# Splitting the accumulating expert scatters of the last 22 tiles into two column halves

## The chip, the cores and the metric

The kernel runs on one core of one Trainium2 chip. The metric is the device time of one launch in microseconds (us). The engines of the core are named as in the profile: PE (TensorE) multiplies matrices, PEld is its weight load, DVE (VectorE) and ACT (ScalarE) work elementwise, POOL (GpSimd) here issues the indirect DMAs, and SP (SyncE) issues the plain ones. An indirect DMA takes an index for each of the 128 partitions and writes that partition's row to the row of a DRAM tensor that the index names; with an add as its compute operation it adds the row to what stands there.

## What is computed

A tokenizer turns the input into 4 x 64 x 64 = 16384 tokens of 256 columns. One attention layer with decay and one MLP follow, and then a mixture of 8 experts, of which every token uses its best two:

```python
logits = tokens @ router_w.T
probs = softmax(logits)
rw, re = top_k(probs, 2);  rw = rw / rw.sum(-1)
combine = zeros(N, E); combine[arange(N), re] = rw
out = tokens
for e in range(8):
    h = gelu(tokens @ w1[e] + b1[e])
    y = h @ w2[e] + b2[e]
    out = out + combine[:, e:e+1] * y
```

The reference evaluates all experts for all tokens; the kernel gathers, for each expert, only the tokens that chose it. Each token's row of the output so receives two additions from expert work, from two different experts, and with that from two different tiles.

## The kernel before

**Blocks.** The tokens are worked on in 32 blocks of 512 (`BLK`), numbered by `Block.i`; `NS` is 31, so the last block is number 31. In one turn of the main loop three blocks are in flight: one is embedded, the middle one goes through attention and MLP, the oldest is routed. When a block is routed, its MLP output is stored to `out` (`Block.store`, the store is kept as `self.stored`), and each token's row of 260 four-byte words (the 256 columns and four words with weights and the token's number) is scattered to `xbuf`, a DRAM buffer with a region for each expert (`Block.scatter`, L814 to L829, a plain indirect DMA at L819).

**Tiles.** After a block is placed, `take` (L858) turns the rows that have piled up into `Tile` objects: 256 rows of one expert. There are 131 of them. The last but one take makes 4 tiles (from block 29), the last take 18 (from block 30). The last block's tokens are not scattered: all 8 experts run on all of them (`Expert`, L1058), and the results are combined in the buffer `h` and stored at the end (L1115).

**A tile's stages.** `load` fetches the expert's weights and the rows, `turn` rearranges them, `enter` (L997) does the first product and the gelu, `leave` (L1014) the second product into a PSUM buffer of the pool `p_tm` (three buffers), and `sums` (L1027) finishes: DVE adds the bias (L1036, out of PSUM into `y`, of which pool `four` has four buffers), multiplies by the token's share (L1038, twice), for the last take's tiles also computes `known` (L1043, the row numbers with the rows that another tile already handled turned away), and then POOL issues two indirect DMAs with an add, one for each 128 of the 256 rows (L1048). `Expert` does the same for the last block with `enter` (L1076, product at L1081) and `leave` (L1092, product at L1098, DVE at L1106 and L1112).

**What sets the order.** SP, PE, DVE and ACT run in the order in which the kernel's source issues the work (`MANUAL`); POOL is not in that list, the compiler's planner places its instructions. Toward the end the loop alternates: an `expert_step` of a tile, a piece of the last block's MLP, another tile; and after the MLP, tiles and the eight `Expert` objects in turn.

**The order of the additions.** An accumulating DMA reads the destination and writes it back. Two tiles of different experts may hold the same token. So the kernel declares the tensor `out` free of automatic dependencies (`unordered`) and states the needed ones itself: both scatters of a tile wait until both scatters of the tile before (`added[-2:]`) and the store of the block (`self.block.stored`) have landed. The scatters of all tiles so form one chain.

Of the kernel before, what the change touches and what calls it, by code (L numbers as in the profile page):

```python
# [13 lines left out]
I32 = mybir.dt.int32  # L14
# [3 lines left out]
ALU = mybir.AluOpType  # L18
AX = mybir.AxisListType

P = 128
# [15 lines left out]
def vit_tower_kernel(  # L37
# [15 lines left out]
    nc = tc.nc  # L53
    B, NBLK, _, XW = x.shape
    D = wtok.shape[2]
# [22 lines left out]
    NS = NB - 1  # L78
# [17 lines left out]
    sums = [p_g.tile([P, BLK], F32, name=f"sums{i}") for i in range(3)]  # L96
# [17 lines left out]
    with tc.tile_pool(name="prep", bufs=1) as prep:  # L114
# [19 lines left out]
        for j in range(J):  # L134
            ps = p_mm.tile([P, 2, D], F32, name="mm")
            for odd in range(2):
                for k in range(CH):
                    n = (odd * CH + k) * 2
# [74 lines left out]
    twelve = ctx.enter_context(tc.tile_pool(name="twelve", bufs=12))  # L213
# [627 lines left out]
    def after(what, others):  # L841
        for other in others:
            tc.add_manual_dep(
                what.ins,
                other.ins.name,
                mybir.DependencyInfo(mybir.DependencyClass.Sync, mybir.DependencyReason.DATA),
                reason="rows",
            )

    def unordered(name, what, others):  # L850

        tc.declare_no_dep(what.ins, group=name, keep=[o.ins for o in others], reason="rows of their own")
        after(what, others)
        tc.add_to_no_dep_group(name, what.ins)
# [93 lines left out]
    AHEAD = 4  # L948
    last_product = [None]
    tiles = []  # L950
    added = []

    class Tile:

# [72 lines left out]
        def sums(self):  # L1027
            w, ps = self.w, self.ps
            share = small.tile([P, 2], F32, name="tile_share")
            tag = w[:, 5 * D + KD : 5 * D + KD + 1]  # L1030
            nc.vector.scalar_tensor_tensor(
                share, self.xg.bitcast(F32)[:, :, FIRST - D], tag, self.xg.bitcast(F32)[:, :, DIFF - D], ALU.is_equal, ALU.mult
            )
            nc.vector.tensor_tensor(share, share, self.xg.bitcast(F32)[:, :, SECOND - D], ALU.add)
            y = four.tile([P, 2, D], F32, name="y")
            nc.vector.tensor_tensor(y, ps, w[:, 4 * D : 5 * D].unsqueeze(1).to_broadcast([P, 2, D]), ALU.add)  # L1036
            for c in range(2):
                nc.vector.tensor_scalar(y[:, c, :], y[:, c, :], share[:, c : c + 1], None, ALU.mult)  # L1038

            number = self.xg[:, :, NUMBER - D : NUMBER - D + 1]  # L1040
            if self.done is not None:
                known = twelve.tile([P, 2, 1], I32, name="known")
                nc.vector.tensor_tensor(known[:, :, 0], number[:, :, 0], self.done[:, self.t, :], ALU.max)  # L1043
                number = known

            before = added[-2:] + [self.block.stored]
            for c in range(2):
                add = nc.gpsimd.indirect_dma_start(  # L1048
                    out=out,
                    out_offset=bass.IndirectOffsetOnAxis(ap=number[:, c, :], axis=0),  # L1050
                    in_=y[:, c, :],
                    in_offset=None,
                    compute_op=ALU.add,
                )
                unordered("sums", add, before)
                added.append(add)

    class Expert:  # L1058

# [63 lines left out]
    at = dict(load=0, fetch=0, turn=0, enter=0, leave=0, sums=0)  # L1123
# [34 lines left out]
    def slot_halves(known, load=True, sums=True):  # L1158

        if len(tiles) - at["enter"] > LEFT and at["enter"] + 2 <= known:  # L1160
            yield from expert_halves(load=load, sums=sums)
# [299 lines left out]
```

## Time and profile before

| | |
|---|---|
| median of three runs | 2114.51 us |
| lowest and highest run | 2113.27 and 2120.39 us |
| the profiled execution's own time | 2116.49 us |
| its span in the profile | 2114.7 us |
| granted TensorE clock | 0.994 |
| busy: PE / PEld / DVE / ACT / POOL | 98% / 75% / 79% / 52% / 42% |
| accumulating scatters (L1048) | 226 + 36 |

The profile is one execution. The span runs from the first to the last instruction; the execution's time has 1.8 us more. Times inside the profile are given from the start of the span. The busy times of the page are over the whole span; since stages differ, what counts here is the last 150 us, for which the trace was asked separately. The profiled duration of an indirect DMA on POOL is the engine's own work on it, not the movement of the data. The name that stands after "<-" for the releaser of a wait is inferred, and where it names an instruction that plainly ended by chance at that moment, the real one is another.

### The profile page before, as it was taken

To read this page: it belongs to the slowest core of one execution; us is meant where nothing else is said; L and a number is where in the kernel's file an instruction comes from. 1 tells how busy PE (TensorE), PEld (TensorE's weight loads), DVE (VectorE), ACT (ScalarE), POOL (GpSimd) and SP (SyncE) were. 2 spreads that over 40 slices of the span, in tenths; PEclk is the share of its full clock that TensorE was granted. 3 is DMA by queue.
4 is the path that set the end of the run, shared out by engine and by line. 5 is a ranking of instruction groups with operands and counts; after the bars stand their busy time and mean duration, and the time that the engine had idled before them with its cause. 6 is when DMAs were issued, how large, how long until landed. Compare 5 with 4: busy or idle time off the path is not lost.

```text
span 2114.7 us, 30454 instructions
## 1 busy us (share of the span) xinstructions
PE 2077.4 (98%) x9042; PEld 1576.0 (75%) x9042; DVE 1674.8 (79%) x5179; ACT 1100.8 (52%) x1966; POOL 886.9 (42%) x768
## 2 busy tenths in 40 slices
PE   8999999999999999999999999999999999998999
PEld 5777677777777777777777777787777787676776
DVE  6778888888888888888888888888888888767445
ACT  2344455655545565554556555455665545543453
POOL 1032234444444444544444444444444444535444
PEclk9999999999999999999999999999999999999999
DMA  4031256766676676567667766766776567688653
GB/s 142 4 123 64 80 131 138 160 143 129 134 157 146 155 160 139 125 143 159 156 143 160 150 122 136 157 156 143 163 157 118 138 149 161 138 197 168 91 69 50
DMA packets 424519, 283.21 MB, mean 134 GB/s; under 512 B 355104, under 2 KB 391072, under 8 KB 420256
## 3 DMA queue, kind: packets, MB, share of 16 engines
q1 hardware_dynamic: 373424, 208.35, 42.5%
q0 software_dynamic: 49632, 67.39, 17.8%
q10 hardware_dynamic: 1296, 5.52, 0.8%
q8 instruction: 71, 1.16, 0.2%
q14 instruction: 96, 0.79, 0.1%
HBM read 118.36 MB, written 86.52 MB: 97 GB/s over the span
## 4 chain that ended last, share of the span: by engine, by line
PE 74%; DVE 11%; ACT 5%; DMA 5%; issue 2%; POOL 2%; SPq 1%; another core or an unknown queue 0%; ACTq 0%; DVEq 0%; POOLq 0%
PE tm L650 17%; PE sums L339 13%; PE tm L396 9%; PE sums L524 9%; PE mm L1002 8%; PE tm L1019 8%; DMA turned<-planes 3%; DVE st L263 2%; PE mm L540 1%; ACT planes L318 1%; ACT tokT L332 1%; PE tm L1098 1%; PE mm L1081 1%; PE mm L539 1%; SPq L326 1%
## 5 line engine op out<-in xcount | busy, mean ns | idle before, releaser
L1048 POOL DMA_INDIRECT out<-y,xg x226 | 369.2, 1634 | 432.7 <-DVE y L1038 220.2
L650 PE MATMUL tm<-w_sb,aT 128*128 128x256 f32 x2048 | 454.7, 380 | 0.0
L339 PE MATMUL sums<-hT,w_sb 128*128 128x512 f32 x1024 | 451.7, 593 | 1.3 <-ACT aT L640 1.3
L650 PEld LDWEIGHTS tm<-w_sb,aT 128*128 128x128 f32 x2048 | 386.7, 190 | 57.2 <-DVE z L611 4.8
L819 POOL DMA_INDIRECT xbuf<-row,to x248 | 257.1, 1037 | 294.3 <-DVE ks L560 170.5
L339 PEld LDWEIGHTS sums<-hT,w_sb 128*128 128x128 f32 x1024 | 193.4, 190 | 219.9 <-issue 201.0
L396 PE MATMUL tm<-wu,xv 128*128 128x256 f32 x1280 | 282.5, 379 | 0.0
L318 ACT COPY planes<-zz 128x1024 uint16<-128x1024 uint16 x100 | 99.3, 1041 | 342.0 <-DVE zz L292 342.0
L396 PEld LDWEIGHTS tm<-wu,xv 128*128 128x128 f32 x1280 | 242.7, 190 | 32.7
L1002 PE MATMUL mm<-xT,w 128*128 128x256 f32 x1048 | 252.5, 384 | 6.9 <-ACT xT L995 3.8
L1019 PE MATMUL tm<-w,ge 128*128 128x256 f32 x1048 | 253.4, 385 | 0.0
L1002 PEld LDWEIGHTS mm<-xT,w 128*128 128x128 f32 x1048 | 201.3, 193 | 49.9 <-issue 16.0
L1019 PEld LDWEIGHTS tm<-w,ge 128*128 128x128 f32 x1048 | 195.9, 191 | 31.4 <-issue 2.9
L640 ACT ACTIVATE aT<-sums,vec 128x512 f32<-128x512 f32 x256 | 167.0, 690 | 60.6 <-PE sums L339 59.3
L995 ACT COPY xT<-xh 128x512 uint16<-128x512 uint16 x262 | 182.1, 767 | 24.4 <-DMA xh<-xbuf 15.4
L283 POOL TENSOR_SCALAR rstd<-mv 128x4 f32<-128x4 f32 x62 | 42.0, 678 | 333.2 <-DVE mv L264 296.7
L1010 ACT ACTIVATE ge<-mm,w 128x256 f32<-128x256 f32 x262 | 109.9, 474 | 137.5 <-PE mm L1002 76.3
L1036 DVE TENSOR_TENSOR y<-tm,w 128x512 f32<-128x512 f32 x131 | 90.6, 691 | 97.9 <-PE tm L1019 86.6
L332 ACT COPY hT<-turned 128x512 uint16<-128x512 uint16 x100 | 66.2, 762 | 80.5 <-DMA turned<-planes 80.5
L263 DVE BATCH_NORM_STATS2 st<-h 128x6 f32<-128x256 f32 x256 | 104.8, 409 | 3.3
L332 ACT COPY tokT<-turned 128x512 uint16<-128x512 uint16 x116 | 76.5, 760 | 58.7 <-DMA turned<-row 58.7
L524 PE MATMUL sums<-hT,wqkv_sb 128*128 128x256 f32 x360 | 107.1, 379 | 0.0
(224 smaller groups left out, 3105.4 us busy)
## 6 DMA issues: line engine op xcount, KB each, us to landing
w<-in_wex SPq DMA_DIRECT2D x113, 641.5 KB
xb<-in_x SPq DMA_DIRECT2D x32, 1040.0 KB
out<-h SPq DMA_DIRECT2D x31, 512.0 KB
bank<-in_wex ACTq DMA_DIRECT2D x8, 641.5 KB
xbuf<-row,to POOLq DMA_INDIRECT x248
out<-y,xg POOLq DMA_INDIRECT x226
xh<-xbuf SPq DMA_TRANSPOSE x131
xg<-xbuf SPq DMA_DIRECT2D x131, 4.0 KB
```

The costliest lines, as they stand in the source:

```text
L263: nc.vector.bn_stats(self.st[:, t, :], src[:, t, :])
L332: copy(to[:, 1 - i], self.turned[:, :, i, k, :])
L339: nc.tensor.matmul(ps, lhsT=w[:, k, ts(m, P)], rhs=rhs[:, k, :], start=k == 0, stop=k == KD - 1)
L396: nc.tensor.matmul(ps[:, n, :], lhsT=xv[:, i, j, :], rhs=wu[:, i, j, :], start=j == 0, stop=j == J - 1)
L524: nc.tensor.matmul(g[:, n, :], lhsT=lhsT, rhs=rhs, start=False, stop=True, skip_group_check=True)
L640: nc.scalar.activation(self.aT[:, m, :], ps, AF.Relu, bias=vec[:, MB1 + m : MB1 + m + 1])
L650: last_product[0] = nc.tensor.matmul(ps[:, i, :], lhsT=self.aT[:, k, ts(u * 2 + i, P)], rhs=w2_sb[:, k, :], start=k == 0, stop=k == KH - 1,)
L819: write = nc.gpsimd.indirect_dma_start(out=xbuf, out_offset=bass.IndirectOffsetOnAxis(ap=self.to[:, c, t : t + 1], axis=0), in_=self.row[: ...
L995: nc.scalar.copy(halves[:, :, :, 1 - i], self.xh[:, i * KD : (i + 1) * KD, :])
L1002: nc.tensor.matmul(ps[:, m, :], lhsT=self.w[:, k * D + m * P : k * D + (m + 1) * P], rhs=self.xT[:, k, :], start=k == 0, stop=k == KD - 1,)
L1019: last_product[0] = nc.tensor.matmul(ps[:, c, :], lhsT=self.ge[:, k, ts(c, P)], rhs=w[:, (2 + k) * D : (3 + k) * D], start=k == 0, stop=k ...
L1048: add = nc.gpsimd.indirect_dma_start(out=out, out_offset=bass.IndirectOffsetOnAxis(ap=number[:, c, :], axis=0), in_=y[:, c, :], in_offset= ...
```

## The change

The tiles of the last two takes (blocks 29 and 30, so 22 of the 131) no longer issue two scatters of 128 rows x 256 columns, but four of 128 rows x 128 columns. For them `out` is viewed as twice as many rows of 128 columns, and two small DVE instructions compute the row numbers of the two halves (2n and 2n + 1). The two scatters of one half wait for the two scatters of the same half of the tile before, no longer for the other half. All other tiles do what they did.

```diff
-    added = []
+    added = [[], []]
...
-            before = added[-2:] + [self.block.stored]
-            for c in range(2):
-                add = nc.gpsimd.indirect_dma_start(
-                    out=out,
-                    out_offset=bass.IndirectOffsetOnAxis(ap=number[:, c, :], axis=0),
-                    in_=y[:, c, :],
-                    in_offset=None,
-                    compute_op=ALU.add,
-                )
-                unordered("sums", add, before)
-                added.append(add)
+            parts = 2 if self.block.i >= NS - 2 else 1
+            if parts == 2:
+                at = twelve.tile([P, 2, 2], I32, name="at")
+                for j in range(parts):
+                    nc.vector.tensor_scalar(at[:, j, :], number[:, :, 0], 2.0, float(j), ALU.mult, ALU.add)
+            befores = [added[j] + [self.block.stored] for j in range(2)]
+            for j in range(parts):
+                adds = []
+                for c in range(2):
+                    index = number[:, c, :] if parts == 1 else at[:, j, c : c + 1]
+                    add = nc.gpsimd.indirect_dma_start(
+                        out=out.rearrange("n (j d) -> (n j) d", j=parts),
+                        out_offset=bass.IndirectOffsetOnAxis(ap=index, axis=0),
+                        in_=y[:, c, ts(j, D // parts)],
+                        in_offset=None,
+                        compute_op=ALU.add,
+                    )
+                    unordered("sums", add, befores[j])
+                    adds.append(add)
+                added[j] = adds
+            if parts == 1:
+                added[1] = added[0]
```

## The prediction

> **What bounds the kernel now.** I read first the busy shares and the end of the chain of waits, then POOL's instructions in order of time, because the change touches only what POOL issues and what waits for it.
>
> ```profile
> PE 2077.4 (98%) x9042; PEld 1576.0 (75%) x9042; DVE 1674.8 (79%) x5179; ACT 1100.8 (52%) x1966; POOL 886.9 (42%) x768
> ```
>
> ```profile
> 2103.07 6.93 PE tm L1098 x32
> ...
> 2110.03 0.70 DVE zz L1106
> ```
>
> The first fence is the page's busy share, the second two steps of the chain that ended last (start, duration, what). PE is busy nearly everywhere, and from 2009.97 to 2110.0 the chain is PE without a gap. Then come the last block's DVE additions, its store, and the span's end at 2114.7. POOL isn't on this chain. So a scatter that lands earlier cannot, by itself, end the kernel earlier.
>
> Next, POOL at the end of the kernel (start, duration, operation, idle before).
>
> ```profile
> 1966.44 1.54 POOL L1048 DMA_INDIRECT out<-y,xg  x1 [3.28 <-DMA out<-y,xg]
> 1968.29 1.54 POOL L1048 DMA_INDIRECT out<-y,xg  x1 [0.30 <-issue]
> ...
> 2060.08 1.54 POOL L1048 DMA_INDIRECT out<-y,known  x1 [3.04 <-DVE known L1043]
> 2061.93 1.54 POOL L1048 DMA_INDIRECT out<-y,known  x1 [0.30 <-issue]
> 2066.42 1.54 POOL L1048 DMA_INDIRECT out<-y,known  x1 [2.95 <-DVE tile_share L1034]
> ...
> 2105.96 1.56 POOL L1048 DMA_INDIRECT out<-y,known  x1 [3.01 <-DVE zz L1106]
> 2107.83 1.78 POOL L1048 DMA_INDIRECT out<-y,known  x1 [0.30 <-issue]
> ```
>
> A tile is two scatters 0.30 us apart and then an idle stretch of about 3 us. The idle is the landing of the pair, whatever name is printed: the DVE instructions named change from tile to tile, while the gap stays. And the data had been there. The scatter at 2060.08 is the 15th of the 22 affected tiles, and DVE had its operands ready long before:
>
> ```profile
> 2048.65 0.62 DVE L1038 TENSOR_SCALAR y<-y,tile_share 128x256 f32<-128x256 f32 x2
> 2049.19 0.15 DVE L1043 TENSOR_TENSOR known<-xg,done 128x2 int32<-128x2 int32 x1
> ```
>
> `y` and `known` were complete at 2049.34, 10.7 us ahead. The same pairing gives 16 us for the first affected tile (ready 1950.2, issued 1966.44) and 4.9 us for the last (ready 2101.08, issued 2105.96). So the scatters are a **chain of their own**, running 5 to 16 us behind the data for the whole tail, at (2105.96 - 1966.44) / 21 = 6.64 us a tile, and ending just in time: POOL ends at 2109.61, the pair lands some 2.9 us later at 2112.5, while the final store sets the end at 2114.7. The slack is 2.2 us. That is the number the change is measured against.
>
> **What the Trainium skill says.** "Perfetto Trace Analysis", section "DMA Instruction — SWDGE (GPSIMD)": the profiled duration of such a DMA ends when the last descriptor is written, not when data has moved. The trace agrees: after the second scatter's end the next tile still waits about 3 us. "DMA: Bandwidth & Descriptors", section "Anatomy of one DMA — SWDGE (gpsimd) path": most of a fixed cost of about 2.0 us is the receipt of the last write. Here it is 2.9 to 3.0 us with the semaphore and the next start; I use the trace. The same page, "SWDGE vs HWDGE vs iDMA": descriptors are computed in software on GpSimd, and an accumulating DMA can be issued nowhere else. So twice the scatters is twice a software job on one engine, unless the job shrinks with the row. No sentence there gives its size by row length. "Rules for kernel authors" there says that an accumulate must wait for an earlier one to the same bytes; the halves keep that, as their bytes are disjoint.
>
> **The change, part by part.** Prices: the group row of L1048 from 1850 us on, the page's row of the plain scatter, and two plain scatters in order of time.
>
> ```profile
> L1048 POOL DMA_INDIRECT out<-y,known x36 | 56.6, 1571 | 63.6 <-DMA out<-y,known 18.9 <-DVE h L1112 10.4 <-DVE tile_share L1034 7.0
> ```
>
> ```profile
> L819 POOL DMA_INDIRECT xbuf<-row,to x248 | 257.1, 1037 | 294.3 <-DVE ks L560 170.5
> ```
>
> ```profile
> 1903.99 0.97 POOL L819 DMA_INDIRECT xbuf<-row,to  x1 [0.30 <-issue]
> 1905.27 0.96 POOL L819 DMA_INDIRECT xbuf<-row,to  x1 [0.30 <-issue]
> ```
>
> *Removed: the landing wait.* The idle column of the first line is 63.6 us for 18 tiles. Less 18 x 0.30 between the two scatters of a pair, 58.2 / 18 = 3.2 us a tile, of which 0.30 is the gap that stands before every scatter and stays; 2.9 are the landing. In the new order a tile issues half 0 twice, then half 1 twice. While half 1 is being issued (2 x 1.87 = 3.7 us), half 0 lands (2.9 us), so the next tile's half 0 finds it landed; likewise for half 1. The wait goes to zero. On POOL that is 22 x 2.9 = 64 us less idle.
>
> *Added: two more scatters a tile.* This is the unknown. The trace shows no accumulating scatter of 512-byte rows. Upper bound: it takes what a 1024-byte row takes, 1.571 us, since there are still 128 indices and 128 rows. Lower bound: half, 0.79 us, if the job were proportional to bytes. I take the **upper**. The plain scatter moves 260 words (1040 bytes) a row, more bytes than the accumulating one, in 0.96 to 1.04 us against 1.57: bytes don't order the two; what is done for each row does. The DMA view agrees that a row is a unit: from 2000 to 2100 us, with 30 scatters,
>
> ```profile
> q0 software_dynamic: 4320, 3.93, 34.2%
> ```
>
> which is 144 packets each, 128 and 16 more, so one per row; halving the columns leaves 128.
>
> The 0.30 us between instructions that wait for nothing stands before every scatter, plain ones too. A tile then costs POOL 4 x (1.571 + 0.30) = 7.48 us, against 6.64 now: it gives up 2.9 us of idle and pays 2 x 1.87 = 3.74.
>
> *The sum.* The first affected tile can't start before 1966.44, since the unchanged tile ahead of it must land first. From there 88 scatters without a pause: 1966.44 + 22 x 7.48 - 0.30 = 2130.7 for POOL's end. Each is late enough for its data: at 7.48 us a tile the last tile is issued at 2123.5, 22 us after its `y` was ready. With 2.9 us of landing the span ends at 2133.6, which is 18.9 us more than 2114.7. The profiled execution took 2116.49 us, 2.0 above the median of the runs; added to the median, 2114.5 + 18.9 = **2133.4, say 2133 us**. With the shortest duration seen (1.542 us) the sum is 2131, with 0.04 us more for a semaphore instruction ahead of each half (44 of them) 2135.
>
> *Two small DVE instructions a tile.* The nearest rows are `known` (0.15 us) and the int32 scalar operations of the norm at 0.17. 44 x 0.17 = 7.5 us of DVE, which in the last 150 us is about half busy (25 of 50 us). Only around 2000.8 to 2005.2, where PE waits for DVE's chain and two tiles' `sums` lie in it, would 4 x 0.2 = 0.8 us be on PE's path. POOL's lateness covers that in the forecast case; without that cover it is 0.8 us.
>
> *The buffers of `y`.* There are four, and DVE's L1036 now waits for all four scatters of the tile four before to have read. Tile k - 4 is issued from 1966.44 + 7.48 (k - 5), takes 7.2 us of POOL and some 2.6 to land, so the release comes at about 1976.2 + 7.48 (k - 5): 2051.0 for k = 15 against 2047.9 today, 2103.4 for k = 22 against 2099.7. DVE is in order, so the last block's additions (L1106) queue behind, and behind these PE, for a PSUM buffer. The waits are up to 4 us, with 2 to 3.7 us of DVE idle beside them today, and they delay PE little; none delays POOL, which has three tiles stored up. I put them at nothing for the end. No other POOL work comes after 1966, so no other queue is moved.
>
> What is late next, then, is POOL itself.
>
> **The rivals.** *(C) Descriptor work shrinks with the row, and the end stays where it is.* The chain would no longer lag, but nothing on the PE chain gets shorter. The point of decision is 1966.44 + 22 p - 0.30 + 2.9 = 2114.7, so p = 6.62 us a tile, 1.36 us a scatter. At 0.79 us a tile costs 4.4 us, the scatters follow the data, and the time is 2114.5 plus at most 0.8: 2115. For it speaks only that no row of the trace excludes it; against it the plain scatter's price. *(B) In between*, 1.36 to 1.50 us, which gives 2115 to 2128. *(D) The halves don't come apart:* the next tile's half 0 also waits for half 1, through a semaphore shared by several scatters or through another order on POOL. A tile would cost 4 x 1.87 - 0.30 + 2.9 = 10.1 us and the kernel end at 1966.44 + 222 = 2188. Against it: plain scatters go out eight in a row at 0.30 us, faster than they could land, so the queue itself doesn't wait.
>
> **How the numbers follow.** Forecast (A) 0.77, B 0.06, C 0.13, D 0.04. About 0.3%, 6.3 us, is what a measurement of this kernel can tell from no change; it corresponds to 6.9 us a tile. A, D and two thirds of B are slower: 0.85. C, save a little, and the rest of B lie within: 0.13. Faster by 6.3 us has no mechanism, as PE's chain ends at 2110; 0.02 for what I don't see. A's own range is 2129 to 2139. The range from 2118 to 2140 adds most of B, and leaves out C and D.
>
> **What would show it.** Right: L1048 groups with 88 scatters at about 1.55 us with idle 0.30 before nearly all of them, POOL near 83% busy after 1966, the chain of waits ending on POOL's L1048, and its last scatter ending about 2130. Right on the buffers: DVE's L1036 waiting for a scatter. Wrong: scatters of half rows well below 1.36 us with idle ahead of them (C), or 3 us gaps still there (D).

## The result and the profile after

The changed kernel takes 2133.07 us in the median of four runs (2131.82 to 2134.96), beside 2114.53 us for the kernel before on the same chip (2113.27 to 2120.39): 18.5 us more, a ratio of 1.0083 with a 95% interval of 1.0063 to 1.0103. The profiled execution took 2132.31 us, and its span is 2130.5 us. The lines moved: the scatter is now L1056, the two new DVE instructions are L1050, the last block's products are L1092 and L1109 and its DVE steps L1117 and L1123.

The page's busy shares:

```profile
PE 2076.1 (97%) x9042; PEld 1576.0 (74%) x9042; DVE 1682.3 (79%) x5223; ACT 1099.1 (52%) x1966; POOL 955.7 (45%) x812
```

PE's work is what it was (2077.4 us before); POOL has 44 instructions and 68.8 us more. POOL is still the least busy of the engines that the page lists, and it is the one that ends the kernel now. The shares of the whole span don't show that; the last stretch does. The last steps of the chain of waits (start, duration, what):

```profile
2120.23 1.50 POOL out L1056
2121.73 0.34 issue
2122.08 1.54 POOL out L1056
2123.62 1.85 POOLq L1468
2125.47 0.30 issue
2125.77 1.54 POOL out L1056
```

Before, these steps were PE's L1098 and DVE's L1106. Now they are one scatter after the other, with 0.30 us between. The scatter at 2123.92 is the step that is named after POOL's queue (POOLq). PE's last group, and POOL in order of time (start, duration, engine, line, what, idle before it in brackets):

```profile
2101.00 3.62 PE L1109 MATMUL tm<-bank,ret 128*128 128x256 f32 x16
```

```profile
1957.47 1.54 POOL L1056 DMA_INDIRECT out<-y,xg  x1 [0.30 <-issue]
1962.30 2.09 POOL L1056 DMA_INDIRECT out<-y,at  x1 [3.29 <-DMA out<-y,xg]
1964.70 1.55 POOL L1056 DMA_INDIRECT out<-y,at  x1 [0.31 <-issue]
1966.55 1.54 POOL L1056 DMA_INDIRECT out<-y,at  x1 [0.30 <-issue]
1968.40 1.54 POOL L1056 DMA_INDIRECT out<-y,at  x1 [0.31 <-issue]
1970.25 1.54 POOL L1056 DMA_INDIRECT out<-y,at  x1 [0.30 <-issue]
...
2123.92 1.54 POOL L1056 DMA_INDIRECT out<-y,at  x1 [0.30 <-issue]
2125.77 1.54 POOL L1056 DMA_INDIRECT out<-y,at  x1 [0.30 <-issue]
```

PE is through at 2104.6, POOL at 2127.3. The 3 us pauses of before end with the first affected tile at 1962.30; from there the 88 scatters follow one another without a pause, (2125.77 - 1962.30) / 87 = 1.879 us each, so 7.52 us a tile against 6.64. The groups of the last stretch (from 1940 us on; count, then busy time, mean ns of one, then idle before and what ended it):

```profile
L1056 POOL DMA_INDIRECT out<-y,at x88 | 138.5, 1574 | 29.8 <-issue 14.3 <-DMA out<-y,at 4.9 <-DMA out<-y,xg 3.3
...
L1036 DVE TENSOR_TENSOR y<-tm,w 128x512 f32<-128x512 f32 x22 | 15.2, 692 | 64.4 <-DMA out<-y,at 40.8 <-PE tm L1019 21.9 <-PE mm L1092 1.5
...
L1050 DVE TENSOR_SCALAR at<-known 128x2 int32<-128x2 int32 x36 | 4.6, 190 | 0.6
L1050 DVE TENSOR_SCALAR at<-xg 128x2 int32<-128x2 int32 x8 | 1.0, 188 | 0.0
```

A scatter of half a row takes 1574 ns; the full row took 1571. And DVE's L1036 now waits 40.8 us for scatters that still hold `y`; in the profile before it has no such wait.

### The profile page after: what moved, and what is told of

Its sections match the earlier page's. It is cut to its first block, busy times and chain, and to the rows that moved or that the text cites. A ratio compares the mean times of both kernels' runs of the same rounds, so it can differ in the third digit from the quotient of the medians.

```text
span 2130.5 us, 30573 instructions
## 1 busy us (share of the span) xinstructions
PE 2076.1 (97%) x9042; PEld 1576.0 (74%) x9042; DVE 1682.3 (79%) x5223; ACT 1099.1 (52%) x1966; POOL 955.7 (45%) x812
## 4 chain that ended last, share of the span: by engine, by line
PE 69%; DVE 12%; DMA 8%; ACT 5%; POOL 3%; issue 2%; SPq 1%; POOLq 0%; DVEq 0%; ACTq 0%
PE tm L650 17%; PE sums L339 13%; PE tm L396 9%; PE sums L524 9%; PE mm L1002 7%; PE tm L1019 7%; DMA turned<-planes 4%; DMA out<-y,at 2%; DVE st L263 2%; POOL out L1056 2%; ACT planes L318 2%; PE mm L540 1%; ACT tokT L332 1%; PE mm L539 1%; SPq L326 1%
## 5 line engine op out<-in xcount | busy, mean ns | idle before, releaser
L1056 POOL DMA_INDIRECT out<-y,xg x218 | 355.5, 1631 | 414.1 <-DVE y L1038 220.8
L339 PE MATMUL sums<-hT,w_sb 128*128 128x512 f32 x1024 | 451.5, 593 | 1.2 <-ACT aT L640 1.2
L819 POOL DMA_INDIRECT xbuf<-row,to x248 | 257.7, 1039 | 291.6 <-DVE ks L560 170.6
L339 PEld LDWEIGHTS sums<-hT,w_sb 128*128 128x128 f32 x1024 | 193.4, 190 | 219.6 <-issue 201.3
L1002 PE MATMUL mm<-xT,w 128*128 128x256 f32 x1048 | 251.7, 383 | 5.0 <-ACT xT L995 5.0
L1002 PEld LDWEIGHTS mm<-xT,w 128*128 128x128 f32 x1048 | 200.6, 192 | 47.1 <-issue 14.7
L995 ACT COPY xT<-xh 128x512 uint16<-128x512 uint16 x262 | 182.0, 766 | 27.2 <-DMA xh<-xbuf 26.6
L1010 ACT ACTIVATE ge<-mm,w 128x256 f32<-128x256 f32 x262 | 109.6, 473 | 133.8 <-PE mm L1002 116.6
L1036 DVE TENSOR_TENSOR y<-tm,w 128x512 f32<-128x512 f32 x131 | 90.5, 691 | 107.6 <-PE tm L1019 64.5
L1056 POOL DMA_INDIRECT out<-y,at x88 | 138.5, 1574 | 29.8 <-issue 14.3
```

The lines of the kernel that those rows point to most:

```text
L339: nc.tensor.matmul(ps, lhsT=w[:, k, ts(m, P)], rhs=rhs[:, k, :], start=k == 0, stop=k == KD - 1)
L819: write = nc.gpsimd.indirect_dma_start(out=xbuf, out_offset=bass.IndirectOffsetOnAxis(ap=self.to[:, c, t : t + 1], axis=0), in_=self.row[: ...
L995: nc.scalar.copy(halves[:, :, :, 1 - i], self.xh[:, i * KD : (i + 1) * KD, :])
L1002: nc.tensor.matmul(ps[:, m, :], lhsT=self.w[:, k * D + m * P : k * D + (m + 1) * P], rhs=self.xT[:, k, :], start=k == 0, stop=k == KD - 1,)
L1056: add = nc.gpsimd.indirect_dma_start(out=out.rearrange("n (j d) -> (n j) d", j=parts), out_offset=bass.IndirectOffsetOnAxis(ap=index, axis=0),
```

## The experiments

The theory: the end is 88 scatters times the price of one, and the price doesn't shrink with the columns. The rivals to be told apart from it: the halves still wait for each other; the time comes from the waits for `y`; it comes from the index work on DVE. A second question is whether the point of decision lies where the prediction put it, and a third why a scatter of half the bytes costs the same. Medians are given with the lowest and highest run; each ratio is to the kernel before on the same chip.

**Halves that wait for both halves.** The four scatters stay, the split wait goes.

```diff
-            befores = [added[j] + [self.block.stored] for j in range(2)]
+            both = added[0] if added[0] is added[1] else added[0] + added[1]
+            befores = [both + [self.block.stored]] * 2
```

> Four half scatters as in the change, but each waits for both halves of the tile before. Theory (POOL's issue work is the bound, and the split did take the landing wait away): a tile now costs 4 x 1.57 + 3 x 0.30 + 2.9 + 0.3 = 10.4 us at most, 10.1 at least, so the tail of 22 tiles takes 222 to 229 us from its first scatter, idle of about 3 us stands ahead of one scatter in four, and the time is about 2187 us. Rival (the landing wait was no part of the period, so taking it away changed nothing): about 2133 us as with the change.

Measured: 2187.65 us (2184.55 to 2188.49), ratio 1.0335 (1.0318 to 1.0351). POOL in order of time (one tile and the start of the next):

```profile
2056.90 1.54 POOL L1057 DMA_INDIRECT out<-y,at  x1 [2.52 <-DMA out<-y,at]
2058.74 1.71 POOL L1057 DMA_INDIRECT out<-y,at  x1 [0.30 <-issue]
2060.76 1.80 POOL L1057 DMA_INDIRECT out<-y,at  x1 [0.30 <-issue]
2062.87 1.54 POOL L1057 DMA_INDIRECT out<-y,at  x1 [0.31 <-issue]
2067.21 1.54 POOL L1057 DMA_INDIRECT out<-y,at  x1 [2.80 <-DVE y L1036]
```

The pause ahead of each tile is back. The change so consists of two terms that can be read apart: four scatters in place of two cost 72.4 us (this kernel against the one before), and the split wait gives 72.4 - 18.5 = 53.9 us back, some 2.5 us a tile. The change does remove what it says it removes. The pauses here are those of half rows, 2.4 to 3.3 us with the 0.30 in them; the full rows of before have 2.8 to 4.0.

**The index work alone.** The two DVE instructions of a tile are kept, the scatters are those of before.

```diff
+            parts = 1
             for j in range(parts):
```

> The two DVE index instructions of each of the 22 tiles are kept, but their result is not used: two full-width scatters as before. Theory: 44 short DVE instructions lie beside other work, time 2114 to 2115.5 us, within 0.1% of before. Rival (the index work stands on the path of the tail and makes part of the 18 us): 2118 us or more.

Measured: 2116.66 us (2114.97 to 2121.02), ratio 1.0010 (1.0002 to 1.0018), so between 0.4 and 3.8 us; that is a little over the 2114 to 2115.5 us expected. At most a fifth of the 18.5 us can come from here. The prediction's 0.8 us lies in the interval, but the profiles say more. PE's longest wait in the last 150 us is the one that the prediction named, for DVE's chain and ACT after it. Before, and here:

```profile
2009.97 3.44 PE L1002 MATMUL mm<-xT,w 128*128 128x256 f32 x8 [3.76 <-ACT xT L995]
```

```profile
2008.69 3.78 PE L1002 MATMUL mm<-xT,w 128*128 128x256 f32 x8 [5.04 <-ACT xT L995]
```

From PE's last group of L339 (24 products) to PE's end it is 161.3 us before and 163.2 here, 1.9 us more. The profiles in which no tile, or only the last eight, have the index work lie at 161.0 to 161.3; the changed kernel, the halves of 64 rows and the scatters with pauses (both below) lie at 163.0 to 163.5. So the place was right, and the price is about 1.9 us.

**Six buffers for `y`.** The change, with two more buffers in memory that is free by then, for every third tile of the last take.

```diff
-            y = four.tile([P, 2, D], F32, name="y")
+            if self.block.i >= NS - 1 and self.t % 3 == 2:
+                spare = wqkv_mix.rearrange("p a b q -> p (a b q)")[:, ts(self.t // 3 % 2, 2 * D)]
+                y = spare.rearrange("p (c d) -> p c d", c=2)
+            else:
+                y = four.tile([P, 2, D], F32, name="y")
```

> The change, with two more buffers for y in the last take (a third of its tiles puts y where the mixed attention weights stood, which are no longer needed then). Theory: DVE's waits for the scatters to have read y (13 of them, 41 us in the changed kernel) shrink to a few us or none, PE ends no later, and the time stays at 2132 to 2134 us, as POOL sets it. Rival (the waits for y hold the tail back): 2 us or more faster than the change.

Measured: 2133.56 us (2132.74 to 2141.57), ratio 1.0098 (1.0079 to 1.0116). The waits of DVE for `y` (total us, times, longest):

```profile
DVE y L1040 <- DMA out<-y,at: 6.8, 2, 5.3
DVE y L1040 <- DMA out<-y,xg: 5.4, 1, 5.4
```

From 40.8 us in 13 waits to 12.2 us in three, more than the few us expected, and the time is that of the change. (The profiled execution took 2141.57 us.) The waits for `y` in the changed kernel so cost the end nothing: they are the lateness of POOL, seen from DVE.

**Only the last eight tiles split.**

```diff
-            parts = 2 if self.block.i >= NS - 2 else 1
+            parts = 2 if self.block.i >= NS - 1 and self.t >= 10 else 1
```

> Only the last 8 tiles are split, the 14 ahead of them keep their two full scatters. Theory: each split tile adds 0.84 us to the chain (7.48 less 6.64), the last one 3.7 in length, and 2.2 us of slack come off: 7 x 0.84 + 3.7 - 2.2 = 7.4 us more than before, about 2122 us. Rival (a cost that comes once, where halves begin or at the end, not per tile): 2133 us as with the change, or no difference.

Measured: 2125.86 us (2120.14 to 2129.65), ratio 1.0047 (1.0030 to 1.0063), so 6 to 13 us. The 7.4 us expected lie in that interval, near its lower end. The time grows with the number of split tiles, as a sum of scatters does.

**Fewer rows at full width.** The kernel before, with 64 rows in each scatter of the 22 tiles.

```diff
+            rows = P // 2 if self.block.i >= NS - 2 else P
...
-                    out_offset=bass.IndirectOffsetOnAxis(ap=number[:, c, :], axis=0),
-                    in_=y[:, c, :],
+                    out_offset=bass.IndirectOffsetOnAxis(ap=number[:rows, c, :], axis=0),
+                    in_=y[:rows, c, :],
```

> The kernel before, but the two accumulating scatters of each of the 22 tiles take only the first 64 of their 128 rows, at full width (the other half of these tiles' additions is left out). It moves the same bytes as a half-width scatter of 128 rows. Theory (the price goes by rows): 0.75 to 0.95 us instead of 1.57. Rival (a price per instruction, whatever it holds): 1.5 us or more. The time says little either way, since the last block's store sets the end: about 2114 us.

Measured: the price is far off.

```profile
2010.12 1.42 POOL L1049 DMA_INDIRECT out<-y,known  x1 [2.46 <-DVE known L1043]
2011.84 1.42 POOL L1049 DMA_INDIRECT out<-y,known  x1 [0.30 <-issue]
```

Half the rows take 1.42 us, not 0.75 to 0.95. What the prediction said of the price, that what is done for each row makes it, doesn't hold. The time was 2105.36 us (2102.71 to 2107.66), ratio 0.9965 (0.9947 to 0.9983): some 8 us faster than before, where no change was expected. These 8 us aren't in the tail: from PE's last group of L339 to PE's end this profile has 161.3 us, as the profile before has. They lie in one stretch ahead of it, from PE's L305 (which transposes the last block for its MLP) to that group. Before:

```profile
1934.73 0.60 PE L305 MATMUL mm<-ident,zz 128*128 128x128 f32 x4
1942.23 3.78 PE L1002 MATMUL mm<-xT,w 128*128 128x256 f32 x8 [2.43 <-ACT hT L306]
1948.66 10.46 PE L339 MATMUL sums<-hT,w_sb 128*128 128x512 f32 x24
```

And with 64 rows:

```profile
1931.57 0.60 PE L305 MATMUL mm<-ident,zz 128*128 128x128 f32 x4
1937.05 10.46 PE L339 MATMUL sums<-hT,w_sb 128*128 128x512 f32 x24
```

The stretch takes 13.9 us before and 5.5 here (the two profiled executions are 11.6 us apart; the other 3 lie further ahead): before, ACT and DVE stand still in it for a while (ACT ahead of its L306 for 2.96 us) and PE with them, and PE's eight products of L1002 after it take 3.78 us, where 1.89 are usual. The same edit with 32 rows shows whether that lasts.

**32 rows at full width.** `P // 4` in place of `P // 2`.

> The kernel before, but the two accumulating scatters of the 22 tiles take only the first 32 rows (three quarters of these tiles' additions are left out). Theory (fixed price and a slope from the two points 1.54 us at 128 rows and 1.42 us at 64): 1.36 us. Rival (fixed below some number of rows): 1.42 us. On the time: the run with 64 rows was some 8 us below before although the tail was as long; if that comes from shorter scatters it comes again here (about 2105 us), if it is chance of one program, the time is about 2114 us.

Measured: 2112.76 us (2111.62 to 2119.67), ratio 1.0000 (0.9988 to 1.0011). The 8 us are not there, and the stretch from L305 to L339 takes 13.9 us again, so they don't come with a shorter scatter. In ten of the thirteen profiles of this document that stretch takes 12.9 to 14.1 us, in the changed kernel's 11.0, and only with 64 rows and with six buffers 5.5 and 5.8. What decides on it was not found. The price:

```profile
2003.92 1.35 POOL L1049 DMA_INDIRECT out<-y,known  x1 [2.25 <-DVE tile_share L1034]
2005.57 1.33 POOL L1049 DMA_INDIRECT out<-y,known  x1 [0.30 <-issue]
```

128, 64 and 32 rows take 1.54, 1.42 and 1.33 us: 2 to 3 ns for each row, on top of some 1.25 us that an accumulating scatter costs whatever it moves. The 1.25 is an estimate (1.33 less 32 x 2.8 ns is 1.24); nothing under 32 rows was measured.

**Halves of 64 rows.** The change, with each of the four scatters cut to its first 64 rows: a quarter of the bytes, and the two reasons for the price crossed.

```diff
-                    index = number[:, c, :] if parts == 1 else at[:, j, c : c + 1]
+                    rows = P // parts
+                    index = number[:, c, :] if parts == 1 else at[:rows, j, c : c + 1]
...
-                        in_=y[:, c, ts(j, D // parts)],
+                        in_=y[:rows, c, ts(j, D // parts)],
```

> The change, but each of the four half scatters takes only the first 64 of its 128 rows (the other rows' additions of the 22 tiles are left out). Theory (POOL sets the end, and an accumulating scatter has a price per instruction with little per row: 1.42 us at 64 rows in the full-width run): a tile costs 4 x (1.42 + 0.30) = 6.88 us, 88 x 0.12 = 10.7 us less than the change, about 2122 us. Rival (half rows of half width, a quarter of the bytes, cost half or less): below the point of decision, about 2114 us.

Measured: 2124.24 us (2120.68 to 2125.95), ratio 1.0043 (1.0028 to 1.0057).

```profile
2114.41 1.42 POOL L1057 DMA_INDIRECT out<-y,at  x1 [0.30 <-issue]
2116.14 1.42 POOL L1057 DMA_INDIRECT out<-y,at  x1 [0.30 <-issue]
```

1.42 us again, with 512 bytes a row as with 1024. The width has no part in the price. And the end follows the price, as in the prediction's sum: with the group's mean of 1.449 us a tile is 4 x (1.449 + 0.30) = 7.0 us, and from 1966.44 the span would end at 1966.44 + 22 x 7.0 - 0.30 + 2.9 = 2123.0, 8.3 us past the span of before. Added to 2114.5 that makes 2122.8; measured are 2124.2. That it fits so closely is in part luck: in this profile the first affected scatter starts 2.9 us earlier than in the sum, and the span ends 4.6 us after POOL's last scatter, not 2.9.

**A chain that no longer lags.** The kernel before, whose 44 scatters in question write plainly.

```diff
-                    compute_op=ALU.add,
+                    **({} if self.block.i >= NS - 2 else dict(compute_op=ALU.add)),
```

> The kernel before, but the two scatters of each of the 22 tiles write instead of adding, at full width (the addition of these tiles is left out). Theory: 0.96 to 1.04 us each as at half width, the scatters follow the data, the last block's store sets the end, 2112 to 2116 us. Rival (what held the half-width plain run at 2123 us comes with plain writes): 2119 us or more.

Measured: 2114.11 us (2107.43 to 2119.09), ratio 0.9996 (0.9987 to 1.0005). POOL in order of time:

```profile
2056.51 0.96 POOL L1048 DMA_INDIRECT out<-y,known  x1 [7.60 <-DVE known L1043]
2057.77 0.96 POOL L1048 DMA_INDIRECT out<-y,known  x1 [0.30 <-issue]
2065.15 0.96 POOL L1048 DMA_INDIRECT out<-y,known  x1 [6.42 <-DVE tile_share L1031]
```

The pauses of 6 to 8 us say that POOL now waits for data: the chain has caught up with DVE. Nothing clear of noise is gained by it; the interval leaves room for less than 3 us. So the kernel before wasn't held by its scatter chain, late as that ran, and a cheaper scatter can't bring the time under that of before by more than that.

**Plain halves.** The change, with plain writes in place of additions.

```diff
-                        compute_op=ALU.add,
+                        **({} if parts == 2 else dict(compute_op=ALU.add)),
```

> The change, but the four half scatters of the 22 tiles write instead of adding (the addition of these tiles is left out). Theory (what is done per row sets the price, and an add costs more per row): a plain half scatter takes what a plain full row takes, 0.96 to 1.04 us, a tile costs 4 x 1.27 = 5.1 us, which is under the point of decision of 6.6; the scatters catch up with the data, the end goes back to the last block's store, about 2115 us. Rival (four scatters cost what they cost whatever they do, or the loss is in DVE's waits for y): 2128 us or more.

Measured: 2122.80 us (2120.14 to 2128.13), ratio 1.0036 (1.0023 to 1.0048). The price is as expected, and POOL waits for data again:

```profile
L1056 POOL DMA_INDIRECT out<-y,at x88 | 87.3, 992 | 68.0 <-DVE at L1050 26.5 <-issue 20.8 <-DVE tile_share L1031 11.6
```

Yet the time misses by 8 us: here PE is late, its last group ending at 2118.8, and from PE's last group of L339 to PE's end it is 172.4 us, where the index work alone has 163.2. Where PE stopped, DVE and ACT had stopped before it. First POOL's last scatter of a row of twelve (a row: scatters with no more than the 0.30 us between them), then one of SP's transposing DMAs, then ACT and DVE:

```profile
1977.74 0.96 POOL L1056 DMA_INDIRECT out<-y,at  x1 [0.30 <-issue]
1979.86 0.00 SPq L972 DMA_TRANSPOSE xh<-xbuf  x1
...
1981.48 0.84 ACT L1010 ACTIVATE ge<-mm,w 128x256 f32<-128x256 f32 x2 [13.75 <-issue]
1981.53 0.69 DVE L1036 TENSOR_TENSOR y<-tm,w 128x512 f32<-128x512 f32 x1 [11.60 <-remote]
```

Twelve plain scatters go out from 1963.56 on, 1.27 us apart. From about 1970 to 1981.5, three microseconds after the last of them, DVE and ACT do nothing, though PE's products for ACT's L1010 were done at 1972.4. SP's issues show 0.00 to 0.01 us in that time, where 0.4 and 1.3 are usual. The busy time in six of these microseconds (the length, then PE, PEld, DVE, ACT and POOL, each with its instructions, then PE's clock, the DMAs' share and GB/s):

```profile
1972.00:1978.00 6.00, 5.12 (x22) 3.72 (x20) 0.00 (x0) 0.00 (x0) 4.39 (x6) 1.00 0.24 64
```

The next row, of twelve again, ends at 2022.55, and DVE starts again at 2024.71 after 8.75 us; after the third, of eight, it has been idle for 3.8 us. The five later rows of eight go without.

**Plain halves in the last take only.** My first reading was a single standstill, near 1975, that had nothing to do with the scatters. Here the four tiles of the last but one take are as before.

```diff
-            parts = 2 if self.block.i >= NS - 2 else 1
+            parts = 2 if self.block.i >= NS - 1 else 1
```

> The four half-width scatters that write instead of adding, now only for the last 18 tiles (their addition is left out); the four tiles ahead keep two full scatters that add. Theory: the 8 us by which the run with 22 such tiles lay above before came from one standstill of DVE and ACT near its first tiles that belongs to no scatter; without it the time is that of before, 2112 to 2117 us. Rival (four writes a tile cost something themselves, through DVE's wait for y or the DMA engines): 2119 us or more.

Measured: 2128.66 us (2125.43 to 2130.93), ratio 1.0050 (1.0034 to 1.0067). The reading fell. There is no standstill near 1975 now, but one at the first unbroken row of the scatters, of twenty, which goes from 1995.34 to 2021.34; DVE starts again 3 us after it:

```profile
2024.47 0.69 DVE L1036 TENSOR_TENSOR y<-tm,w 128x512 f32<-128x512 f32 x1 [14.73 <-remote]
```

From L339 to PE's end it is 171.7 us.

**Plain scatters with pauses.** Every other tile is split, and all scatters of a tile wait for all of the tile before, so that a row is never longer than four.

```diff
-            parts = 2 if self.block.i >= NS - 2 else 1
+            last = self.block.i >= NS - 2
+            parts = 2 if last and self.t % 2 == 0 else 1
...
-            befores = [added[j] + [self.block.stored] for j in range(2)]
+            both = added[0] if added[0] is added[1] else added[0] + added[1]
+            befores = [both + [self.block.stored]] * 2
...
-                        **({} if parts == 2 else dict(compute_op=ALU.add)),
+                        **({} if last else dict(compute_op=ALU.add)),
```

> The 22 tiles of the last two takes write plainly instead of adding (left out: these tiles' additions). Tiles with an even number are split into halves, the others are full width, and each tile waits for all scatters of the tile before, so a pause of about 3 us stands ahead of every tile and never more than four scatters follow one another 0.30 us apart. Theory (the 8 us and 10 us that the plain halves cost in two earlier kernels come from the standstill of SP, ACT and DVE during eight or more plain scatters without a pause): a tile costs 4 x 1.27 + 2.7 = 7.8 us or 2 x 1.27 + 2.7 = 5.2 us, 6.5 us in the mean, just under the pace of the data, the standstill is gone, and the time is that of the kernel before, 2112 to 2117 us. Rival (the cost belongs to each split plain scatter or to its index work, wherever it stands): half or more of the plain halves' cost remains, 2119 us or more, and DVE or ACT still stand still for over 8 us after 1970.

Measured: 2116.40 us (2113.24 to 2119.70), ratio 1.0003 (0.9994 to 1.0011).

```profile
2027.75 0.96 POOL L1058 DMA_INDIRECT out<-y,at  x1 [2.59 <-DMA out<-y,known]
2029.01 0.96 POOL L1058 DMA_INDIRECT out<-y,at  x1 [0.30 <-issue]
2030.27 0.95 POOL L1058 DMA_INDIRECT out<-y,at  x1 [0.30 <-issue]
2031.53 0.96 POOL L1058 DMA_INDIRECT out<-y,at  x1 [0.30 <-issue]
2034.75 0.96 POOL L1058 DMA_INDIRECT out<-y,known  x1 [2.26 <-DVE tile_share L1034]
```

There is no standstill among these scatters, the time is that of before, and from L339 to PE's end it is 163.0 us. It has half as many split scatters as the plain halves, so that a cost of each would have left 4 us, a ratio of 1.0018, and the interval excludes that. So the loss of the plain halves goes with long rows: after those of twelve and of twenty there is a standstill, and with pauses between every four there is none. But a long row isn't enough. The five later rows of eight show nothing, and in every kernel here POOL goes through the same row of twelve near 1920 to 1940 (four scatters with an add and the eight plain ones of L819), next to the stretch that takes 13.9 us before and 5.5 us in the run with 64 rows. The changed kernel's own 88 scatters, in one row 1.85 us apart, bring no such standstill, so that its 18.5 us have nothing to do with this. What in the chip brings it about was not found.

No edit of these scatters made the tail shorter than it was before. With PE's chain as the bound, the best that a change to them reached is no change; the one lower time, with 64 rows, comes from ahead of them.

## Why the prediction was right, step by step

**The bound.** PE's chain to 2110, with the scatter chain close behind, was right. The kernel whose chain caught up with DVE takes 2114.11 us, and the one with 32 rows 2112.76, both with intervals that hold no change. The slack of 2.2 us was not measured by itself. Not all of that chain is work, though: the 8 us of standing still near 1940 lie ahead of the part that the prediction looked at, and it passed over them.

**The landing wait removed.** Right in kind: no pause is left in the trace after. In size it was put at 2.9 us a tile, which is what the full rows of before show; against the kernel with joint waits, whose halves land sooner, it is some 2.5. That kernel gave 2187.65 us where rival (D) said 2188. The size did no harm, since a wait that goes to zero enters the sum only through the end: the sum was made from the instructions that stay.

**Two more scatters a tile.** Put at 1.571 + 0.30 us, measured 1.574 + 0.30, and POOL is busy 138.5 us of the 166 from 1962 to 2128, 83% as foreseen. This term alone decides the result. The value was right; **the reason for it was wrong.** The prediction took the upper bound because "what is done for each row does" order the prices. The runs with 64 and 32 rows show 1.42 and 1.33 us: most of the price comes with the instruction. Splitting by columns keeps rows and doubles instructions, so that both reasons give the same number here, and that the wrong one was enough is luck; a split by rows would have been mispriced by it at half. The argument that the plain scatter moves more bytes in less time spoke against bytes, and nothing in it spoke for rows rather than for the instruction. The packets did not either: an accumulating scatter does send one a row and 16 more (144, 80 and 48 for 128, 64 and 32 rows, from the pages' totals, and 144 again for a half row), but a third of the packets takes 14% less time.

**The start and the end of the sum.** Put at 1966.44 for the first affected scatter, it came at 1962.30 in the profile after, 4.1 us earlier. 88 x 0.008 us for the slightly longer step and 0.3 us of longer landing (3.2 from POOL's end to the end of the span, where 2.9 were put) give 1.0 back, and the span is 2130.5 where 2133.6 was the sum. The start belongs to the execution and not to the change: in the three other profiles in which the same 22 tiles issue four accumulating scatters each, and whose source differs in nothing ahead of that, it is 1963.51 (halves of 64 rows), 1966.15 (joint waits) and 1971.06 (six buffers). That the sum of the span misses by 3 us and the difference of the medians by only 0.4 is luck in part. Between medians the change costs 18.5 us where the sum said 18.9.

**The index instructions.** 0.19 us each beside an estimate of 0.17, 5.6 us of busy time since pairs overlap. Their cost on PE's chain was put at 0.8 us, at the right place, and is about 1.9 us in the profiles: this term was mis-sized. POOL's lateness covers it, as foreseen.

**The buffers of `y`.** They were foreseen as waits up to 4 us, at no cost for the end: the longest is 5.5 us, and taking two thirds of them away changes nothing. PE's only gap over 0.3 us after 1942 is one of 5.0 us at 2003.6, at ACT's L995, where the profile before has 3.8 and the index work alone 5.0.

**The rivals.** (C) and (B) hung on a scatter under 1.36 or under 1.50 us. The price doesn't fall with the columns at all, so neither could come. With 64 rows of half width the price falls to 1.42, and the time lands in (B)'s stretch, at 2124.

## What to carry to other kernels

Before splitting an indirect DMA, measure what issuing one costs its engine: here a scatter with an add costs POOL 1.3 to 1.5 us with 32 to 128 rows, and the two more that split the wait cost 3.7 us a tile and save some 2.5. Work out at which price per step such a chain overtakes the bound, and ask whether the new instruction's price comes with its bytes, its rows or with itself; one run with fewer rows tells. When a time moves that shouldn't, compare the same stretches of two profiles before explaining it: the run with 64 rows was 8 us faster for a reason ahead of everything that was edited. A busy share says nothing of this: the engine that ended the kernel is the least busy of those that the page lists.

## What was not expected of the hardware

An accumulating scatter's time on POOL is 1.54, 1.42 and 1.33 us for 128, 64 and 32 rows, and the same for rows of 512 and 1024 bytes; a plain one of 128 rows takes 0.96. The Trainium skill says in "DMA: Bandwidth & Descriptors", section "SWDGE vs HWDGE vs iDMA", that software on GpSimd computes the descriptors; these runs show that, from 32 to 128 rows, most of that time doesn't depend on how many rows there are. Nor does it follow the packets: 48 of them take 1.33 us with an add (32 rows) and 0.96 us in a plain scatter of 128 full rows.

Rows of twelve and of twenty plain scatters without a pause went with a standstill of DVE, 8.8 to 14.7 us long, that ended 2 to 3 us after the last of them, and with times 8 and 10 us above that of before. Four in a row, with 2 to 3 us of pause, had none, and neither had 88 accumulating ones without a pause, nor five later rows of eight. In the kernel before, ACT and DVE stand still in a like way near 1940, beside a row of twelve with eight plain ones, and the run with 64 rows has that row without it and is 8 us faster. Whether the two are one thing, and why, is open.
